# Attention softmax by single steps instead of doubles, with reciprocals ahead of older turns and x loads regrouped

## The chip, the cores and the metric

The kernel runs on one core of one Trainium2 chip. The metric is the device time of one execution in microseconds (us). The engines of the core run side by side, each through its own queue in order: TensorE (PE in the profile; its weight loads are PEld), VectorE (DVE), ScalarE (ACT), GpSimd (POOL) and SyncE (SP). SP computes nothing here; it issues most of the DMAs, POOL issues some. An instruction that waits holds up what is behind it on its own queue. PSUM is the memory into which TensorE writes[...]; SBUF is the memory that the others share.

## What is computed

Two layers on x, 4 images of 16 x 16 positions with 1024 channels, that is, 1024 tokens in 4 batches of 256. Everything is in float32. Layer 0 is a group norm, a convolution-like attention and a residual. Layer 1 is what the change is about, followed by a mixture of 8 experts:

```python
t = t + attn(ln(t), W_attn, b_attn, W_proj, b_proj)
...
qkv = einsum('btc,oc->bto', x, W_attn) + b_attn      # 16 heads of 64
att = einsum('bhqd,bhkd->bhqk', q, k) * (1.0 / sqrt(64))
att = where(causal, att, -1e29)
att = softmax(att, axis=-1)
y = einsum('bhqk,bhkd->bhqd', att, v)
y = einsum('btc,oc->bto', y, W_proj) + b_proj
```

## The kernel before

The stages follow each other: layer 0; layer norm and its turn (transposition of the rows); the products for v; then the stage of the change, attention with the q and k projections woven in; then the second layer norm, gating and lists; then the experts.

**The attention stage.** The 16 heads go as 8 pairs of heads. One pair in one batch is a *single step*: two heads, 256 queries, 256 keys. Two single steps are a *double*, and there are 16 doubles (`doubles`, lines 927 and 928): for the first six pairs a double is one pair in two batches, for the last two pairs it is both pairs in one batch. What happens to a double:

- `scores(d)` (line 817): TensorE writes q times k into one PSUM tile of four banks (line 824). VectorE adds the causal mask (838), takes two negated row maxima (843) and scales them (844). ScalarE takes eight exponentials into the SBUF tile s_q, with the row sums in total (848).
- `scored(d)` (858): VectorE takes the reciprocal of the sums (860), POOL multiplies s_q by it in eight pieces (863). SP then writes s_q to DRAM as one DMA of 768 KB (869) and reads it back by four DMAs of 192 KB (873) into s_rows, the quarters rearranged. The reads wait for the write.
- `turned(d)` (876): VectorE transposes s_rows in blocks of 32 x 32 into s_T (878).
- `values(d)` (884): TensorE multiplies v by s_T into the PSUM tile pa (891), VectorE adds the bias into y_T (900 or 909).

The tiles psc, s_q, s_rows and s_T have one buffer each, of the size of a double.

**The order.** The loop at line 940 is written out by hand (`manual_schedule`) and holds with step d work of three doubles: the turn of d - 2, the reciprocal, products and DMAs of d - 1, and the values of d - 2 and the scores of d. Each engine's order is the order of the text. Around these stand *units*: a unit is one of the seven products (in Strassen's way, on half-size blocks) of one pair's q and k projection, `project_qk` (779), four matmuls of 128 x 512 and an eviction on VectorE or ScalarE. A pair's product 4 is followed by the four sums of weights for the next pair, on VectorE (lines 160 to 163). `upto` (931) says how many units a step holds: 4, 3, 4, 3, 4, 4, 4, 4, 4, 3, 3, 5, 3 and 1 for steps 1 to 14. The units go through the PSUM tags mm and tr, two banks each; pa and the output projection use the same tags.

In each step the first two units come first, then the turn of d - 2, then the reciprocals and the DMAs of d - 1, then the other units, then values and scores. From step 14 on there are no units left and the output projection takes their place: `project_out(t, j)` (914), eight matmuls for 128 tokens and half of the columns, with `values_and_scores` called after its sixth. It adds its result to the tokens of x, which have been written to DRAM (x_rows) before and are loaded again in eight tiles of 512 KB by POOL's queue (968), two in step 14, two in step 15, four in step 16. Their SBUF space is that of the sums T and S of the projections, which must be done with. The weights of the output projection come in two halves, w_p0 in step 12 and w_p1 in step 14, on SP. Behind the loop (step 17 is the last) the gating stage begins; its first instructions on ScalarE and POOL wait until the last pa matmul is done, since they use that stage's space.

Of the kernel before, what the change touches and what calls it, by code (L numbers as in the profile page):

```python
# [32 lines left out]
F32 = mybir.dt.float32  # L33
# [6 lines left out]
P = 128  # L40
C = 1024
NC = C // P
# [3 lines left out]
NT = TOK // P  # L46
# [16 lines left out]
Q = 4  # L63
# [6 lines left out]
def kernel(  # L70
# [29 lines left out]
    def pool(stack, name, bufs=1, **kw):  # L100
        return stack.enter_context(tc.tile_pool(name=name, bufs=bufs, reuse_waits="tile", **kw))
# [545 lines left out]
    with ExitStack() as attention:  # L647
# [168 lines left out]

        def scores(d):

            psc = ps.tile([P, 4, HALF], F32, tag="sc", name=f"sc{d}", bufs=1)
            for k, (pair, b) in enumerate(doubles[d]):  # L820
                for qt in (1, 0):
                    for h in range(2):
                        part = slice(h * D, h * D + D)
                        nc.tensor.matmul(
                            psc[:, 2 * k + h, qt * P : qt * P + (qt + 1) * P],
                            qk[pair][part, 0, b * M + qt * P : b * M + (qt + 1) * P],
                            qk[pair][part, 1, b * M : b * M + (qt + 1) * P],
                            start=True,
                            stop=True,
                        )  # L830

            by_quarter = l1w.tile([P, Q, 12, 32], F32, tag="s_q", name=f"s_q{d}", bufs=1)

            def blocks(k, qt):
                return by_quarter[:, :, 3 * k + qt : 3 * k + 1 + 2 * qt, :].rearrange("p f b i -> p b f i")

            last = psc.rearrange("p k (t n) -> p k t n", t=2)[:, :, :, :P]
            nc.vector.tensor_add(last, last, mask.unsqueeze(1).unsqueeze(1).to_broadcast([P, 4, 2, P]))
            top = small.tile([P, 2, 4], F32, tag="top", name=f"top{d}")
            total = small.tile([P, 2, 4], F32, tag="total", name=f"total{d}")  # L840
            for qt in range(2):
                cols = slice(qt * P, qt * P + (qt + 1) * P)
                nc.vector.tensor_reduce(top[:, qt, :], psc[:, :, cols], AX.X, ALU.max, negate=True)
            nc.vector.tensor_scalar(top, top, 1.0 / D**0.5, None, ALU.mult)  # L844
            for k in range(4):
                for qt in range(2):
                    cols = slice(qt * P, qt * P + (qt + 1) * P)
                    nc.scalar.activation(  # L848
                        blocks(k, qt),
                        psc[:, k, cols].rearrange("p (b f i) -> p b f i", f=Q, i=32),  # L850
                        AF.Exp,
                        bias=top[:, qt, k : k + 1],
                        scale=1.0 / D**0.5,
                        accum_out=total[:, qt, k : k + 1],
                    )
            return blocks, total, by_quarter

        def scored(d, blocks, total, by_quarter):

            nc.vector.reciprocal(total, total)  # L860
            for k in range(4):
                for qt in range(2):
                    nc.gpsimd.tensor_mul(  # L863
                        blocks(k, qt),
                        blocks(k, qt),
                        total[:, qt, k : k + 1].unsqueeze(2).unsqueeze(3).to_broadcast([P, 1 + qt, Q, 32]),
                    )
            rows = turns.tile([P, Q, 12 * 32], F32, tag="rows", name=f"s_rows{d}")
            nc.sync.dma_start(rows.rearrange("q f r -> q (f r)"), by_quarter.rearrange("p f b i -> p (f b i)"))

            s_rows = l1w.tile([P, Q, 12 * 32], F32, tag="s_rows", name=f"s_rows{d}", bufs=1)
            for f in range(Q):
                nc.sync.dma_start(s_rows[ts(f, 32), :, :], rows[:, f, :].rearrange("(g j) r -> j g r", j=32))
            return s_rows

        def turned(d, s_rows):
            s_T = l1w.tile([P, 4, 3 * P], F32, tag="s_T", name=f"s_T{d}", bufs=1)
            nc.vector.transpose(  # L878
                s_T.rearrange("p k (b g j) -> p g (k b) j", b=3, g=Q),
                s_rows.rearrange("p g (b i) -> p g b i", i=32),  # L880
            )
            return s_T

        def values(d, s_T):

            pa = mm(f"pa{d}").rearrange("p (k n) -> p k n", k=2)
            for k, (pair, b) in enumerate(doubles[d]):
                g, off = pair // 2, (pair % 2) * P
                for kt in range(2):
                    for h in range(2):  # L890
                        nc.tensor.matmul(
                            pa[h * D : h * D + D, k, kt * P :],
                            v1[g][:, 2 * b + kt, off + h * D : off + (h + 1) * D],
                            s_T[:, 2 * k + h, 2 * kt * P : (kt + 2) * P],
                            start=(kt == 0),
                            stop=(kt == 1),
                        )
            (pair, b), (other, _) = doubles[d]
            if pair == other:
                nc.vector.tensor_scalar(  # L900
                    y_T[:, pair, b * M : (b + 2) * M],
                    pa.rearrange("p k n -> p (k n)"),
                    bv[:, pair : pair + 1],
                    None,
                    ALU.add,
                )
            else:
                for k, (pair, b) in enumerate(doubles[d]):
                    nc.vector.tensor_scalar(y_T[:, pair, ts(b, M)], pa[:, k, :], bv[:, pair : pair + 1], None, ALU.add)
# [17 lines left out]
        doubles = [((pair, b), (pair, b + 1)) for pair in range(pairs_in_turn) for b in (0, 2)]  # L927
        doubles += [((NPAIR - 2, b), (NPAIR - 1, b)) for b in range(B)]
        queue = [(pair, n) for pair in range(1, NPAIR - 2) for n in (1, 2, 6, 7, 4, 5, 3)]
        queue += [(pair, n) for some in ((1, 2, 6, 7, 4), (5, 3)) for pair in (NPAIR - 2, NPAIR - 1) for n in some]  # L930
        upto = (0, 4, 7, 11, 14, 18, 22, 26, 30, 34, 37, 40, 45, 48, 49)
        units = {d: queue[upto[d - 1] : upto[d]] for d in range(1, len(upto))}
        outs = {14: ((0, 0), (1, 0)), 15: ((2, 0), (0, 1)), 16: ((1, 1), (2, 1)), 17: ((3, 0),)}
        lag = 2
# [4 lines left out]
        with tc.manual_schedule():  # L939
            for d in range(len(doubles) + lag):  # L940
                if d % 4 == 0 and d < 12:
                    load_qk(d // 4 + 1)
                elif d == 12:
                    w_p.append(w_tile("w_p0", W_projT[:, :HALF]))

                def values_and_scores():
                    if d >= lag:
                        values(d - lag, turned_s.pop(d - lag))
                    if d < len(doubles):
                        made[d] = scores(d)  # L950

                ahead = units.get(d, ())
                for unit in ahead[:2]:
                    project_qk(*unit)
                if d >= lag:
                    turned_s[d - lag] = turned(d - lag, soft.pop(d - lag))
                if d - 1 in made:
                    soft[d - 1] = scored(d - 1, *made.pop(d - 1))
                for unit in ahead[2:]:
                    project_qk(*unit)  # L960
                if d == 14:
                    w_p.append(w_tile("w_p1", W_projT[:, HALF:]))
                    sums.close()
                    x_pool = pool(x_home, "xb", side="right")
                    xs = [x_pool.tile([P, C], F32, tag=f"x{t}", name=f"xb{t}") for t in range(NT)]
                    bp = pool(bp_home, "bp", side="right").tile([P, C], F32, tag="bp", name="bp")
                for t in {14: (0, 1), 15: (2, 3), 16: (4, 6, 5, 7)}.get(d, ()):
                    nc.gpsimd.dma_start(xs[t], x_rows[ts(t, P), :])
                if d == 15:
                    nc.gpsimd.dma_start(bp, b_proj.partition_broadcast(P))  # L970
                if d == 17:
                    for b, nt in tiles[NT - 2 :]:
                        nc.gpsimd.tensor_add(xs[2 * b + nt], xs[2 * b + nt], bp)
                if d in outs:
                    project_out(*outs[d][0], {NC - 3: values_and_scores}, True)
                    for out_of in outs[d][1:]:
                        project_out(*out_of, {}, True)
                else:
                    values_and_scores()
        share_banks("ps_rest", 3)  # L980
        bp_home.close()

# [738 lines left out]
```

## Time and profile before

| | us |
|---|---|
| median of 3 runs (lowest, highest) | 1237.92 (1236.72, 1238.04) |
| the profiled execution | 1239.31 |
| its span, first to last instruction | 1237.5 |
| attention loop, first scores to the end of the last values | 389.1 to 669.3 |
| VectorE busy in 389 to 671.2 | 152.8 of 282.2 |
| granted TensorE clock, mean of the span | 0.997 |

Mean durations in that stage: one 128 x 1536 transpose (878) 1775 ns; mask 1231 ns; the two maxima 691 and 1214 ns; one exponential 374 (128 x 128) or 484 ns (128 x 256), and 215 ns to read each sum; one eviction of 128 x 512 about 690 ns. From issue to landing, in the median, a write of s_q takes 3.3 us and a read of a quarter 3.8 us.

How to read the profile: an instruction's line is that of the kernel, and "x8" behind a row is how often it stands there. A float32 matmul leaves two records, so a unit is x8, values and scores x16. "[3.14 <-DMA s_rows<-s_rows]" means that the engine sat idle for 3.14 us before the instruction, and what ended that. A row of SPq or POOL with DMA_DIRECT2D is the issue of a DMA, not its transfer.

### The profile page before, as it was taken

The page shows a single profiled execution, that of the slowest core. Times are in us where ns is not written, and L with a number is a line of the kernel's source. Part 1 is how long each engine was busy: PE and PEld are TensorE (multiplying, and loading weights), DVE is VectorE, ACT ScalarE, POOL GpSimd, SP SyncE. Part 2 cuts the span into 40 slices and gives each one's busy share as a digit, 9 for nine tenths or more (in the row PEclk, how much of TensorE's full clock was granted, in tenths as well). Part 3 has the DMA queues.
Part 4 walks back from the last instruction along what each step waited for, and adds up shares of the span by engine and source line. Part 5 has one row for each costly group of instructions (what it writes and reads, how often), then busy time and mean ns, then how long its engine had stood idle before and what let it go on. Part 6 is the DMA issues. An engine that isn't in the chain of part 4 may idle for free.

```text
span 1237.5 us, 12955 instructions
## 1 busy us (share of the span) xinstructions
PE 1210.2 (98%) x4780; PEld 633.8 (51%) x4780; DVE 713.6 (58%) x1178; ACT 201.7 (16%) x502; POOL 404.5 (33%) x467
## 2 busy tenths in 40 slices
PE   9999999999999999999988999999999999999998
PEld 5445885778874445444443444444344434434443
DVE  5796636757323566566543567666656556565642
ACT  3310111120001222221210221101201111111110
POOL 0051341354000222133232016436442635364521
PEclk9999999999999999999999999999999999999999
DMA  9002014772210353535466755574855575556442
GB/s 348 24 1 77 10 50 141 242 249 69 68 53 15 103 170 102 171 102 168 126 191 179 250 175 186 153 222 89 239 144 158 111 229 162 142 147 183 100 83 54
DMA packets 82599, 169.75 MB, mean 137 GB/s; under 512 B 10688, under 2 KB 39376, under 8 KB 82528
## 3 DMA queue, kind: packets, MB, share of 16 engines
q1 hardware_dynamic: 62080, 108.48, 27.6%
q0 software_dynamic: 16144, 51.45, 17.3%
q10 hardware_dynamic: 4304, 8.91, 2.1%
q8 instruction: 40, 0.66, 0.2%
q14 instruction: 31, 0.25, 0.1%
HBM read 116.12 MB, written 48.50 MB: 133 GB/s over the span
## 4 chain that ended last, share of the span: by engine, by line
PE 81%; DMA 9%; DVE 3%; POOL 2%; issue 2%; SPq 2%; ACT 1%; DVEq 0%; POOLq 0%; ACTq 0%
PE p L1487 31%; PE pqk L665 13%; PE pv L665 7%; PE pq_pair L400 4%; PE left L1529 3%; PE pq L319 3%; PE pT L510 3%; DMA s_rows<-s_rows 3%; PE pk L431 2%; DMA ln_rows<-ln_rows 2%; PE pv L538 2%; DMA s_rows<-s_q 2%; POOL s_q L863 2%; PE rest L1543 2%; DMA quarters<-rows 2%
## 5 line engine op out<-in xcount | busy, mean ns | idle before, releaser
L1012 POOL DMA_INDIRECT w_e_xg<-rows,gather x146 | 155.5, 1065 | 50.9 <-issue 42.0
L1487 PE MATMUL p<-w_e,A 128*128 128x512 f32 x368 | 163.2, 593 | 1.3 <-DVE slot L1299 1.3
L863 POOL TENSOR_TENSOR s_q<-s_q,total 128x128 f32<-128x128 f32 (+1 forms) x128 | 63.6, 532 | 283.1 <-DVE total L860 283.1
L918 PE MATMUL po<-w_p,y_T 128*128 128x512 f32 x256 | 116.7, 606 | 0.0
L1035 POOL DMA_INDIRECT out_dram<-y,add x32 | 57.3, 1790 | 178.9 <-ACT y L1493 112.5
L1487 PEld LDWEIGHTS p<-w_e,A 128*128 128x128 f32 x368 | 69.6, 190 | 89.9 <-issue 89.0
L1487 PE MATMUL p<-T,S 128*128 128x512 f32 x256 | 112.7, 593 | 0.0
L1493 ACT ACTIVATE y<-y,slot 128x512 f32<-128x512 f32 x64 | 46.0, 721 | 331.1 <-DVE y L1501 152.7
L665 PE MATMUL pqk<-ln,w_qk 128*128 128x512 f32 x192 | 85.7, 595 | 0.0
L848 ACT ACTIVATE s_q<-sc,top 128x128 f32<-128x128 f32 (+1 forms) x128 | 51.8, 429 | 173.2 <-DVE top L844 101.4
L1487 PEld LDWEIGHTS p<-T,S 128*128 128x128 f32 x256 | 48.6, 190 | 60.8 <-issue 60.8
L918 PEld LDWEIGHTS po<-w_p,y_T 128*128 128x128 f32 x256 | 47.8, 193 | 54.5 <-issue 53.5
L187 DVE STREAM_TRANSPOSE A<-w_e_xg 128x1024 f32<-128x1024 f32 x32 | 39.6, 1238 | 48.6 <-DMA w_e_xg<-rows,gather 48.2
L665 PEld LDWEIGHTS pqk<-ln,w_qk 128*128 128x128 f32 x192 | 36.1, 190 | 43.7 <-issue 42.6
L665 PE MATMUL pqk<-T,S_qk 128*128 128x512 f32 x128 | 58.0, 595 | 0.0
L1487 PE MATMUL p<-T,A 128*128 128x512 f32 x128 | 57.5, 592 | 0.0
L1487 PE MATMUL p<-w_e,S 128*128 128x512 f32 x128 | 57.5, 592 | 0.0
L665 PE MATMUL pv<-w_v,ln 128*128 128x256 f32 x192 | 43.7, 380 | 2.1 <-ACT ln L223 1.1
L319 PE MATMUL pq<-w_q,xn 128*128 128x512 f32 x96 | 44.5, 600 | 0.3 <-ACT xn L299 0.3
L878 DVE STREAM_TRANSPOSE s_T<-s_rows 128x1536 f32<-128x1536 f32 x16 | 28.4, 1775 | 27.3 <-DMA s_rows<-s_rows 27.3
L1529 PE MATMUL left<-w_e,one 128*32 128x512 f32 x312 | 41.8, 593 | 0.0
L665 PEld LDWEIGHTS pv<-w_v,ln 128*128 128x128 f32 x192 | 36.2, 190 | 7.7 <-ACT ln L223 1.3
(329 smaller groups left out, 1823.5 us busy)
## 6 DMA issues: line engine op xcount, KB each, us to landing
w_e<-in_expert_w_dram SPq DMA_DIRECT2D x12, 2048.0 KB, 14.7
s_rows<-s_q SPq DMA_DIRECT2D x16, 768.0 KB, 3.3
s_rows<-s_rows SPq DMA_DIRECT2D x64, 192.0 KB, 3.8
w_qk<-in_W_attnT_dram SPq DMA_DIRECT2D x8, 1024.0 KB, 9.3
w_e<-in_expert_w_dram ACTq DMA_DIRECT2D x4, 2048.0 KB, 12.6
xn<-in_xT_dram SPq DMA_DIRECT2D x8, 512.0 KB, 7.2
w_q<-in_Wq_dram SPq DMA_DIRECT2D x16, 256.0 KB, 6.8
x_at<-in_x_dram POOLq DMA_DIRECT2D x8, 512.0 KB
```

The source lines that it names most:

```text
L187: nc.vector.transpose(row_T[:, :, :slots].rearrange("p c (g j) -> p g c j", j=32), row[:, : slots // 32, :].rearrange("p g (c i) -> p g c ...
L319: nc.tensor.matmul(pq, xn[:, c, ts(t, P)], w_q[kc][:, c, :], start=(c == 0), stop=(c == NC - 1))
L400: nc.tensor.matmul(bank, a[:, c, :], b[:, c, :], start=(c == 0), stop=(c == NC // 2 - 1))
L665: nc.tensor.matmul(bank, stationary(c), moving(c), start=(c == 0), stop=(c == NC // 2 - 1))
L848: nc.scalar.activation(blocks(k, qt), psc[:, k, cols].rearrange("p (b f i) -> p b f i", f=Q, i=32), AF.Exp, bias=top[:, qt, k : k + 1], sc ...
L863: nc.gpsimd.tensor_mul(blocks(k, qt), blocks(k, qt), total[:, qt, k : k + 1].unsqueeze(2).unsqueeze(3).to_broadcast([P, 1 + qt, Q, 32]),)
L918: nc.tensor.matmul(po, y_T[:, c, ts(t, P)], w_p[j][:, c, :], start=(c == 0), stop=(c == NC - 1))
L1012: nc.gpsimd.indirect_dma_start(out=row[:, g, :], out_offset=None, in_=table[: (TOK - P) * Q, :] if e in SHORT else table, in_offset=bass.I ...
L1035: nc.gpsimd.indirect_dma_start(out=out[: TOK - P, :] if e in SHORT else out, out_offset=bass.IndirectOffsetOnAxis(ap=add[:slots, e, k : k ...
L1487: nc.tensor.matmul(bank, a[:, c, :], b[:, c, :], start=(c == 0), stop=(c == NC // 2 - 1))
L1493: nc.scalar.mul(y[i][:, ts(j, HALF)], y[i][:, ts(j, HALF)], slot[:, e, 1, 2 * pair + i : 2 * pair + i + 1])
L1529: nc.tensor.matmul(bank[ts(i, 32), :], stationary, w[of][j][:, c, :], start=(c == 0), stop=(c == NC - 1))
```

## The change

- A double stays the unit of TensorE's products: the values, and the scores called for in one go. But the scores go into two PSUM tiles of two banks (tag sc, two buffers instead of one), and the softmax, the multiplication, the DMAs and the transposes go by single steps. s_q, s_rows and s_T have half the size and two buffers.
- A double thus has two writes of 384 KB and eight reads of 96 KB in place of one write and four reads, with the four reads of the first single step ahead of the write of the second on SP's queue. It has two reciprocals and two transposes, and VectorE's mask, maxima and scale twice at half the size.
- In steps 1 to 13 the turn of d - 2 comes after the first unit, not after the second.
- The last units are put in the order (6, 5), (7, 5), (6, 3), (7, 3); step 13 has two, step 14 two.
- In step 14 the reciprocals and DMAs of 13 come ahead of the turn of 12. The turn of 13 comes behind the first output projection of step 14, then the reciprocals of 14; the reciprocals of 15 come behind the second projection of step 15 and ahead of the turn of 14. In step 16 the values come with its second projection, not with its first.
- x is loaded as 0 and 1 in step 13, 2 and 3 in step 14, 4 and 6 in step 15, 5 and 7 in step 16.

The diff, cut to its core (`turned` and `values` follow the new names):

```diff
         def scores(d):
-            psc = ps.tile([P, 4, HALF], F32, tag="sc", name=f"sc{d}", bufs=1)
-            for k, (pair, b) in enumerate(doubles[d]):
+            banks = [ps.tile([P, 2, HALF], F32, tag="sc", name=f"sc{d}_{k}", bufs=2) for k in range(2)]
+            for psc, (pair, b) in zip(banks, doubles[d]):
...
+            return [softmax(f"{d}_{k}", psc) for k, psc in enumerate(banks)]
+
+        def softmax(name, psc):
+            by_quarter = l1w.tile([P, Q, 6, 32], F32, tag="s_q", name=f"s_q{name}")
...
+        def scored(name, blocks, total, by_quarter):
             nc.vector.reciprocal(total, total)
-            for k in range(4):
+            for h in range(2):
                 for qt in range(2):
                     nc.gpsimd.tensor_mul(
...
-            rows = turns.tile([P, Q, 12 * 32], F32, tag="rows", name=f"s_rows{d}")
+            rows = turns.tile([P, Q, 6 * 32], F32, tag="rows", name=f"s_rows{name}")
...
-        queue += [(pair, n) for some in ((1, 2, 6, 7, 4), (5, 3)) for pair in (NPAIR - 2, NPAIR - 1) for n in some]
-        upto = (0, 4, 7, 11, 14, 18, 22, 26, 30, 34, 37, 40, 45, 48, 49)
+        queue += [(pair, n) for some in ((1, 2, 6, 7, 4), (5,), (3,)) for pair in (NPAIR - 2, NPAIR - 1) for n in some]
+        upto = (0, 4, 7, 11, 14, 18, 22, 26, 30, 34, 37, 40, 45, 47, 49)
...
+                def go_on(at):
+                    if at - 1 in made:
+                        soft[at - 1] = [scored(*one) for one in made.pop(at - 1)]
+
+                def turn_back(at):
+                    if at >= lag:
+                        turned_s[at - lag] = [turned(*one) for one in soft.pop(at - lag)]
...
-                for unit in ahead[:2]:
-                    project_qk(*unit)
-                if d >= lag:
-                    turned_s[d - lag] = turned(d - lag, soft.pop(d - lag))
-                if d - 1 in made:
-                    soft[d - 1] = scored(d - 1, *made.pop(d - 1))
-                for unit in ahead[2:]:
-                    project_qk(*unit)
...
-                for t in {14: (0, 1), 15: (2, 3), 16: (4, 6, 5, 7)}.get(d, ()):
-                    nc.gpsimd.dma_start(xs[t], x_rows[ts(t, P), :])
...
+                if d < 14:
+                    for unit in ahead[:1]:
+                        project_qk(*unit)
+                    turn_back(d)
+                    go_on(d)
+                    for unit in ahead[1:]:
+                        project_qk(*unit)
+                    if d == 13:
...
+                        load_x(0, 1)
+                    values_and_scores(d)
+                elif d == 14:
+                    project_qk(*ahead[0])
+                    go_on(14)
+                    project_qk(*ahead[1])
+                    turn_back(14)
+                    w_p.append(w_tile("w_p1", W_projT[:, HALF:]))
+                    load_x(2)
+                    project_out(*outs[14][0], {NC - 3: lambda: values_and_scores(14)}, True)
+                    turn_back(15)
+                    project_out(*outs[14][1], {}, True)
+                    go_on(15)
+                    load_x(3)
+                elif d == 15:
+                    nc.gpsimd.dma_start(bp, b_proj.partition_broadcast(P))
+                    project_out(*outs[15][0], {NC - 3: lambda: values_and_scores(15)}, True)
+                    project_out(*outs[15][1], {}, True)
+                    go_on(16)
+                    load_x(4, 6)
+                    turn_back(16)
+                elif d == 16:
+                    project_out(*outs[16][0], {}, True)
+                    load_x(5, 7)
+                    project_out(*outs[16][1], {NC - 3: lambda: values_and_scores(16)}, True)
+                    turn_back(17)
```

## The prediction

> **What bounds the kernel now.** I read the page's engine line first, then TensorE's own waits, then the busy windows of the stretch in which those waits lie, then the timeline of that stretch.
>
> ```profile
> PE 1210.2 (98%) x4780; PEld 633.8 (51%) x4780; DVE 713.6 (58%) x1178; ACT 201.7 (16%) x502; POOL 404.5 (33%) x467
> PE pa L891 <- DVE s_T L878: 7.6, 3, 5.0
> PE pa L891 <- DVE total L860: 4.0, 2, 3.0
> ```
>
> TensorE is busy for all but 27.3 us of the 1237.5 us span, and the change adds and removes no matmul. So it can only pay in TensorE's idle time and in its clock. The two wait lines (total, times, longest) say where that is: 11.6 us, five times, in front of the attention values (pa, line 891). Both lines are one thing: the values wait for the turned probabilities s_T, and where the wait is put down to the reciprocal (line 860), it is only the instruction behind the transpose on VectorE.
>
> The windows hold steps 14, 15, 16 and 17 of the loop (columns: busy us of PE, PEld, DVE, ACT, POOL with instructions, granted clock, DMA share, GB/s):
>
> ```profile
> 591.48:608.70 17.22, 15.20 (x81) 7.94 (x81) 8.77 (x14) 3.33 (x16) 5.90 (x13) 1.00 0.32 92
> 608.70:626.40 17.70, 16.78 (x65) 8.25 (x64) 7.87 (x12) 3.33 (x16) 4.72 (x11) 1.00 0.90 262
> 626.40:646.00 19.60, 16.56 (x63) 7.93 (x59) 8.80 (x15) 4.81 (x18) 4.89 (x11) 0.99 0.61 166
> 646.00:671.20 25.20, 20.18 (x53) 9.28 (x54) 6.94 (x14) 1.33 (x2) 10.80 (x16) 0.87 0.53 146
> ```
>
> TensorE idles 2.0, 0.9, 3.0 and 5.0 us there; the fifth wait (0.6 us) is at 558.2, in step 11. The clock falls too. In stretches of 4 us it was 0.94 from 642, 0.63 from 646 and 0.57 from 666, after the two longest waits, and 1.00 elsewhere: 4 x (0.06 + 0.37 + 0.43) = 3.4 us. After the waits of 2.0 and 0.9 us it stayed at 1.00. At stake: 11.6 + 3.4 = **15.0 us**.
>
> Why the values wait shows in the last two steps:
>
> ```profile
> 642.39 1.78 DVE L878 STREAM_TRANSPOSE s_T<-s_rows 128x1536 f32<-128x1536 f32 x1 [3.14 <-DMA s_rows<-s_rows]
> 644.09 0.16 DVE L860 RECIPROCAL total<-total 128x8 f32<-128x8 f32 x1
> 644.32 1.68 PE L891 MATMUL pa<-s_T,v 128*64 128x256 f32 x16 [3.04 <-DVE total L860]
> 644.39 3.75 POOL L863 TENSOR_TENSOR s_q<-s_q,total 128x128 f32<-128x128 f32 x8 [14.71 <-DVE total L860]
> ...
> 648.09 2.16 POOL L968 DMA_DIRECT2D xb<-x_rows  x4
> 648.17 0.34 SPq L869 DMA_DIRECT2D s_rows<-s_q  x1
> ...
> 652.84 2.36 SPq L873 DMA_DIRECT2D s_rows<-s_rows  x4
> ...
> 664.60 1.78 DVE L878 STREAM_TRANSPOSE s_T<-s_rows 128x1536 f32<-128x1536 f32 x1 [7.61 <-DMA s_rows<-s_rows]
> ...
> 666.44 2.83 PE L891 MATMUL pa<-s_T,v 128*64 128x256 f32 x16 [5.02 <-DVE s_T L878]
> ```
>
> The reciprocal of double 15 stands on VectorE behind the transpose of double 14, which waits for its DMA. ScalarE had finished the exponentials of 15 at 636.2 (its last record of them), so double 15 lost 8 us by standing in that place. Then its DMAs ran into four x loads: write 4.67 us, reads 11.76 us until the transpose. A loop results: reciprocal, POOL products, write, four reads, transpose, next reciprocal. Its undisturbed length:
>
> ```profile
> 591.58 0.16 DVE L860 RECIPROCAL total<-total 128x8 f32<-128x8 f32 x1
> 591.82 3.75 POOL L863 TENSOR_TENSOR s_q<-s_q,total 128x128 f32<-128x128 f32 x8 [11.89 <-DVE total L860]
> 595.60 0.34 SPq L869 DMA_DIRECT2D s_rows<-s_q  x1
> 598.92 1.73 SPq L873 DMA_DIRECT2D s_rows<-s_rows  x4
> 604.61 1.78 DVE L878 STREAM_TRANSPOSE s_T<-s_rows 128x1536 f32<-128x1536 f32 x1 [4.61 <-DMA s_rows<-s_rows]
> 606.31 0.16 DVE L860 RECIPROCAL total<-total 128x8 f32<-128x8 f32 x1
> ```
>
> 4.02 to the write, 3.32 for it, 5.69 for the reads, 1.70 for the transpose: 14.73 us. A step of TensorE lasts 16.9 us with four projection products (13.93 + 1.45 values + 1.51 scores), 13.46 with three, 20.3 with five.
>
> **Part 1: single steps in the softmax and the turns.** Per double the same elements go through twice the instructions. VectorE: mask 1.23, two maxima 1.82, scale 0.17 become 2 x about (0.65 + 1.05 + 0.17), 0.5 us more; a second reciprocal, 0.16; two transposes of about 0.9 (a 128x1024 one took 1.25), nothing. VectorE idles 130 us of the 282 us of this stage, which hides it. POOL and ScalarE have the same pieces in halves.
>
> The DMAs are the price. SP issues write 0, four reads 0, write 1, four reads 1 in order, and the reads wait for their write, so write 1 stands behind it. A write of 384 KB isn't in the trace. Bounds: half of 3.32, or 3.32 unchanged. A write of 512 KB (rows<-row at 670.58) let its reads go after 3.15, so I take 3.0. [...] For the last read's landing after the four issues, 128 KB reads took 2.84 (675.46 to 678.30), the present 192 KB ones 3.96; I take 2.7 for 96 KB, with 3.96 above it[...].
>
> New loop: 0.24 + 1.88 (half the POOL work) + 0.04 = 2.16 to write 0; 3.0; issues 1.73 and 0.05; write 1 3.0; issues 1.73; landing 2.7; last transpose 0.9: **15.25 us**, 0.5 longer than now[...]. The second half of the values needs its half of s_T 0.7 us after the first, so TensorE tolerates that much more.
>
> Is it short enough? Step 2 (from 405.96) opens with product 4 and its 3.9 us of sums, so its reciprocals come at 416.1, as now. Adding 15.25 a step gives 431.4, 446.6, 461.9, 477.1, 492.4, 507.6 for steps 3 to 8, against values at 433.3, 446.8, 463.7, 480.6, 497.5, 514.4. Steps 9 and 10 are bound by their first product (523.5, 540.4), then 555.7 and 570.9 against 558.2 and 578.5. In step 13 (now two products, from 581.5) they come at 588.3 for values at 588.5. Steps 4 and 13 are tight: I charge 0.5 us there; the 0.6 us wait of step 11 goes. While a transpose waits, the evictions of products 2 to 4 stand behind it on VectorE. Four banks turn over, each reused four products later (13.7 us), so TensorE does not follow. At one product earlier in the order (part 2) the transposes are also off the 9.5 us floor of now (reciprocal 591.58, step from 582.1); the new floor is about 6.2.
>
> **Part 2: the order of the last steps.** In step 14 the reciprocals of 13 stand in front of the transposes of 12, later ones behind a projection but never behind their predecessor's late DMA. Step 14 starts at 591.5. Reciprocals of 12 came at 588.3; their last transpose would be done at 603.5, for values at 603.7. x loads 0 and 1, issued behind POOL's products at 592.3, lie in between. Now, such a pair made the write 4.76 instead of 3.32 and the reads 7.30 instead of 5.69, 3.1 us in all; here only part of the DMAs meets it: 0 to 3.1, I take a wait of **1.0**. Double 13: its writes queue on SP behind 12's last reads (601), turned by about 616, values at 622. Double 14: reciprocals 617, turned by 634 with w_p1 in flight, values at 645. Double 15: reciprocals 634 (now 644), write 0 636, reads 639, write 1 641, with the x loads 645, reads until 650 (alone) to 656 (delayed as now); values at 653.5, half of them 0.7 later. Wait 0 to 2.5; I take **0.7**.
>
> **Part 3: x in smaller portions.** Loads 4, 6 and 5, 7 are two groups in the text, but nothing on POOL waits between them, so they go back to back as now. Only their place changes: 638 instead of 648, behind the products of 15. Issues cost POOL 0.55 each with nobody behind. Units (6, 5) and (7, 5) move ahead of both (3), which frees T for x 0 and 1 in step 13. No cost on TensorE.
>
> **Sum.** 15.0 - 0.5 - 1.0 - 0.7 = **12.8 us**. Short waits cost no clock by the rows above. The profiled execution took 1239.31 (span 1237.5 and 1.8 around it); it would take 1226.5. It lies 1.4 above the median of the runs, 1237.92, which gives **1225.1**.
>
> **Rivals.**
> - *The last turn still meets the x loads* (chance 0.15). If the reads of double 15 again need 11.8 us from about 646, s_T is there at 659 and TensorE waits 4.5 us and loses 1.7 in clock: 1225.1 + 5.5 = about 1230.6. For: the load order is unchanged in effect. Against: the first half's DMAs are ahead of the loads.
> - *The loop over SP becomes the bound* (0.12; slower). Steps 2 to 12 average 15.95 us. A loop of L us costs 11 x (L - 15.95). The 12.8 us are gone at L = 17.1, which is 1.9 above my sum. Two turns of now took 16.5 and 17.2 us (from 526.85 and 558.70), when POOL needed 5.5 instead of 3.75 beside VectorE's sums of weights. At L = 17.7 it costs 19: about 1244. Against: the reciprocals now come before those sums in steps 7 and 9.
> - *The change doesn't remove the waits, merely moves them* (0.05): double 13's DMAs behind 12's on SP push 14 and 15 back until all four waits return: about 1238. Against: 5 to 10 us of margin for 13 and 14.
>
> **The numbers.** The forecast's own case has 0.68 and reaches from 1222.5 (all 15.0 us and noise) to 1228. The range goes to 1233, to hold the first rival and loops a little too long. By over 0.2% (2.5 us, about what a measurement of this kernel can tell from no change): faster 0.84 (0.68 + 0.15 and a hundredth of the loop), within 0.05, slower 0.11 (the rest of the loop).
>
> **What would show it.** Right: TensorE's waits at pa under 3 us; clock 1.00 through the stage; scores and values of step 13 ending near 591; last values near 654 instead of 666; second transposes about 5 us behind first ones; reciprocal to reciprocal at 15 to 15.5 us in steps 3 to 8. Wrong: equal waits of one to two us in every step of three products (the loop), write 1 over 4 us undisturbed, or one long wait in front of the last values.

## The result and the profile after

| | before | after |
|---|---|---|
| median of 4 runs each, side by side (us) | 1237.98 | 1224.81 |
| lowest, highest | 1236.72, 1240.94 | 1222.15, 1227.45 |
| ratio, 95% interval | | 0.989 (0.986 to 0.992) |
| profiled execution, its span | 1239.31, 1237.5 | 1227.45, 1225.6 |
| first scores to the first POOL instruction behind the last values | 389.01 to 669.34 = 280.3 | 389.32 to 655.90 = 266.6 |

The changed kernel is 13.2 us faster. In a second comparison, with five rounds, the ratio was 0.9875 (0.9853 to 0.9898). The last row of the table is the length of the attention stage in the profile; it is free of what other stages do, and I use it below to tell kernels apart. It fell by 13.7 us.

The engine line of the page after, and the two rows of its DMA issues that belong to the change (size of each, median us from issue to landing):

```profile
PE 1208.7 (99%) x4780; PEld 632.8 (52%) x4780; DVE 721.4 (59%) x1274; ACT 203.8 (17%) x502; POOL 401.5 (33%) x467
...
s_rows<-s_q SPq DMA_DIRECT2D x32, 384.0 KB, 2.3
s_rows<-s_rows SPq DMA_DIRECT2D x128, 96.0 KB, 2.3
```

TensorE's idle time is 16.9 us instead of 27.3. VectorE has 7.8 us more work, 0.49 per double, and it hid it all. A write of half the size lands in 2.3 us, where the whole one took 3.3.

TensorE's waits after: the row that heads the list now, which lies behind the stage, and the only one at pa:

```profile
PE lists L1287 <- POOL entry L1276: 2.8, 3, 1.9
...
PE pa L893 <- DVE s_T L880: 0.9, 2, 0.6
```

Of the 11.6 us in front of pa, 0.9 are left, both in step 14 (0.30 and 0.56 us, one for each half). The windows of steps 14 to 17, cut at the same instructions as before (columns as before; the clock is the number ahead of the DMA share):

```profile
591.78:608.11 16.33, 15.47 (x63) 7.59 (x61) 7.93 (x17) 3.44 (x16) 6.03 (x13) 1.00 0.68 218
608.11:625.00 16.89, 16.89 (x67) 8.28 (x65) 8.42 (x18) 3.44 (x16) 4.81 (x10) 1.00 0.76 249
625.00:645.79 20.79, 20.79 (x50) 9.03 (x48) 10.33 (x24) 4.93 (x18) 8.78 (x14) 1.00 0.59 183
645.79:657.60 11.81, 11.81 (x54) 5.83 (x54) 5.13 (x10) 1.33 (x2) 3.46 (x4) 1.00 0.40 123
```

Span and busy time of PE agree from 608.11 on, and the clock is 1.00 in all four. The last values start at 654.31 instead of 666.44.

SP's own rows of double 15, the last one. They show what is left of the trouble with the x loads:

```profile
636.66 0.34 SPq L871 DMA_DIRECT2D s_rows<-s_q  x1
639.05 1.73 SPq L875 DMA_DIRECT2D s_rows<-s_rows  x4
640.88 0.85 SPq L871 DMA_DIRECT2D s_rows<-s_q  x1
649.84 1.73 SPq L875 DMA_DIRECT2D s_rows<-s_rows  x4
```

The reads wait for their write, so the distance between a write's row and the next row is that write's time. Write 0 took 2.39 us. POOL began to issue the four x loads at 638.46; write 1, from 640.88, took 8.96 us. In steps 1 to 12 write 1 took 2.57 to 3.09 us, 2.65 in the median. The second half of s_T was ready at 654.54, half a microsecond before its matmuls were due.

### The profile page after: what moved, and what is told of

Its sections match the earlier page's. It is cut to its first block, busy times and chain, and to the rows that moved or that the text cites. A ratio compares the mean times of both kernels' runs of the same rounds, so it can differ in the third digit from the quotient of the medians.

```text
span 1225.6 us, 13283 instructions
## 1 busy us (share of the span) xinstructions
PE 1208.7 (99%) x4780; PEld 632.8 (52%) x4780; DVE 721.4 (59%) x1274; ACT 203.8 (17%) x502; POOL 401.5 (33%) x467
## 4 chain that ended last, share of the span: by engine, by line
PE 87%; DMA 7%; DVE 3%; SPq 2%; issue 1%; ACT 1%; POOL 0%; DVEq 0%; POOLq 0%; ACTq 0%
PE p L1516 31%; PE pqk L665 15%; PE pv L665 7%; PE po L920 5%; PE pq_pair L400 4%; PE left L1558 3%; PE pq L319 3%; PE pT L510 3%; DMA ln_rows<-ln_rows 2%; PE pk L431 2%; PE sc L824 2%; PE pa L893 2%; PE rest L1572 2%; PE pv L538 2%; DMA quarters<-rows 1%; DMA s<-two_T 1%
## 5 line engine op out<-in xcount | busy, mean ns | idle before, releaser
L865 POOL TENSOR_TENSOR s_q<-s_q,total 128x128 f32<-128x128 f32 (+1 forms) x128 | 60.2, 506 | 276.5 <-DVE total L862 276.5
L1516 PEld LDWEIGHTS p<-w_e,S 128*128 128x128 f32 x128 | 24.3, 190 | 30.6 <-issue 30.1
L1516 PEld LDWEIGHTS p<-T,A 128*128 128x128 f32 x128 | 24.3, 190 | 30.6 <-issue 30.1
```

What stands on the lines that cost most here:

```text
L865: nc.gpsimd.tensor_mul(blocks(h, qt), blocks(h, qt), total[:, qt, h : h + 1].unsqueeze(2).unsqueeze(3).to_broadcast([P, 1 + qt, Q, 32]),)
L1516: nc.tensor.matmul(bank, a[:, c, :], b[:, c, :], start=(c == 0), stop=(c == NC // 2 - 1))
```

## The experiments

Ratios are to the kernel before on the same chip in the same comparison, with the 95% interval. "Stage" is the length defined above: 280.3 us before, 266.6 after.

**1. The order alone, whole doubles.** Functions of the kernel before, loop of the changed kernel:

```diff
-soft[at - 1] = [scored(*one) for one in made.pop(at - 1)]
+soft[at - 1] = scored(at - 1, *made.pop(at - 1))
-turned_s[at - lag] = [turned(*one) for one in soft.pop(at - lag)]
+turned_s[at - lag] = turned(at - lag, soft.pop(at - lag))
```

> The whole doubles of the kernel before, with one buffer each, in the order of the changed kernel (units, reciprocals ahead of older turns, places of the x loads). Theory A, the order of the last steps gives the gain: most of it stays. Two of TensorE's waits at pa should come back in part, because a whole double meets the x loads with all of its DMAs: in step 14, 0.5 to 2.4 us; in front of the last values, 2 to 3 us (reciprocals 634.5, write at 638.3 with the x loads beside it, 4.7 for the write and 11.8 to the transpose as in the kernel before, turned at 656.4 for values planned at 654.3), with up to 1 us of clock. 1224.8 + 3.5 = about 1228 us, from 1225 to 1231. Theory B, the cutting into single steps gives it: the waits at pa return to about 10 us or more, 1235 us or above.

Measured: 1231.41 us, ratio 0.994 (0.9924 to 0.9957), stage 273.2. TensorE's waits at pa:

```profile
PE pa L891 <- DVE s_T L878: 5.2, 2, 3.0
```

The two waits are where they were expected, 2.96 us in step 14 and 2.28 in front of the last values. The clock fell behind both, by 3.4 us in 4 us windows together (0.69 and 0.88 in 604 to 612, 0.57 in 660 to 664), more than I had allowed. A wait of 0.8 us for ScalarE in step 6 is new. The time lies just above the range that I had given. So most of what theory A said holds, but the order alone is worth 7.2 us of the 13.7, and the cutting is worth something too.

**2. The single steps alone, old order.** Functions of the changed kernel, `queue`, `upto` and loop of the kernel before.

> The single steps of the changed kernel, with two buffers each, in the order of the kernel before (two units ahead of the turns, turns of d-2 ahead of the reciprocals of d-1 everywhere, x loads in steps 14 to 16). Theory A, the order gives the gain: the reciprocals of 15 stand behind both transposes of 14 again, the second of which comes 4.5 us behind the first, so the reciprocals come at 644 or later, the writes meet four x loads, and the last values wait 5 us or more, with clock lost behind it: 1236 to 1242 us, as before or slower. Theory B, the single steps give it: waits at pa under 3 us, 1228 us or less.

Measured: 1232.83 us, ratio 0.9948 (0.993 to 0.9966), stage 274.4. This lies between my two theories, and A's number was wrong: single steps help in the old order too, by 5.9 us. Waits at pa are 5.5 us in all (the longest 3.51, the last half of the last values), and a new one of 1.78 us stands in front of an output projection, for w_p1: SP issued that load at 619.32, behind more DMAs. The reciprocals of 15 did come late, at 641.8, and write 0 started at 644.0, before the x loads of 645.8, but its reads already met them. Only 0.9 us separated the first half of the last values from its plan; the second half was the late one.

**3. One pair of the order undone.** In step 15:

```diff
-                    go_on(16)
-                    load_x(4, 6)
-                    turn_back(16)
+                    turn_back(16)
+                    go_on(16)
+                    load_x(4, 6)
```

> The changed kernel with one pair swapped: in step 15 the reciprocals, products and DMAs of double 15 stand behind the transposes of 14 again, and so do the x loads 4, 6, 5, 7. Theory A, the reciprocal's place is what removed the longest wait: reciprocals at 639.1 instead of 634.5, write 0 at 641.2, write 1 at 645.4 beside the x loads (8.9 us as in the changed kernel), reads, landing and transpose until 658.4; the last values, planned at 654.3 and by halves 0.7 later, wait 3 to 3.7 us, and 0 to 2 us of clock go with it: about 1229 us, from 1227 to 1231. Theory C, the place does not matter as long as the DMAs are cut: no wait, 1225 us.

Measured: 1228.87 us, ratio 0.992 (0.9902 to 0.9937), stage 270.1, 3.5 longer than after. TensorE's rows at the end of the stage:

```profile
653.17 0.87 PE L893 MATMUL pa<-s_T,v 128*64 128x256 f32 x8
657.60 0.87 PE L893 MATMUL pa<-s_T,v 128*64 128x256 f32 x8 [3.56 <-DVE s_T L880]
```

The first half is in time, the second waits 3.56 us, as theory A worked out. The reciprocals stood at 637.4 here, write 1 took 9.0 us once more. Where the reciprocal of 15 stands is worth 3.5 us by itself.

**4. Both writes ahead of all reads.** In the changed kernel, `scored` ends behind its write, and the reads follow for both single steps:

```diff
-soft[at - 1] = [scored(*one) for one in made.pop(at - 1)]
+written = [scored(*one) for one in made.pop(at - 1)]
+soft[at - 1] = [read_back(*one) for one in written]
```

> The changed kernel with both writes of a double issued ahead of its eight reads on SP, instead of write, reads, write, reads. My step on the price: write 1 stands behind the four reads of single step 0, so this order shortens the loop by about 1.8 us (write 1 issued at 4.0 us behind the reciprocal, when the POOL products are done, landing at about 7; reads 1 done issuing at 9.0, landed at 11.7, turned at 12.6 instead of 14.4). VectorE's waits for s_rows in steps 3, 5 and 11 (now 4.6, 4.9 and 0.5 us for both transposes) fall by 1.5 to 2 us each, the last transpose of a double comes 2 to 3 us behind the first instead of 4.2 to 4.5. On TensorE only the 0.9 us of waits in step 14 can go: 1224 us, from 1223 to 1225.5, not to be told from the changed kernel. Rival: two writes in flight share the DMA engines, write 0 lands about 1 us later, and the loop keeps its length; the time is the same, 1224.8.

Measured: 1223.51 us, ratio 0.9878 (0.9861 to 0.9894), stage 265.7, no wait at pa. SP's rows of one loop:

```profile
415.60 2.20 SPq L871 DMA_DIRECT2D s_rows<-s_q  x2
418.00 5.09 SPq L878 DMA_DIRECT2D s_rows<-s_rows  x8
```

The reads may go 2.40 us after the first write (2.46 in the changed kernel). But SP issued the second write only at 417.46, when POOL's products for it were done, so the two were in flight together for 0.54 us; what two writes cost each other over their whole length, no run here shows. This loop had its reciprocals at 413.46 and 425.87, 12.4 us apart (14.45 in the changed kernel for the same pair of doubles), and the second transpose came 2.2 us behind the first. In step 5, the other loop in which VectorE waited for both transposes, it was 13.1 against 14.7. The price of SP's order is thus real, 1.6 to 2.0 us a loop, and almost nothing waits for it: the time is that of the changed kernel.

**5 and 6. A longer loop.** The reads issued twice, for both single steps of a double (5, shown here) or for the first alone (6, where the doubling has the condition `name.endswith("_0")`); same data, same place:

```diff
-            for f in range(Q):
+            for f in 2 * tuple(range(Q)):
```

> The changed kernel with the four reads of every single step issued twice (the same data into the same place), to lengthen the loop over SP by what eight more issues take, 2 x 1.73 = 3.5 us. The rival of my prediction that is slower says: in the changed kernel the loop is 14.4 us from reciprocal to reciprocal where nothing disturbs it, TensorE's steps 2 to 12 average 15.95, so a loop of 17.9 us costs 11 x (17.9 - 15.95) = 21 us: about 1246 us, from 1238 to 1256, with waits at pa in nearly every step from 3 to 13, of 1 to 5 us, and more clock lost. If TensorE is not near this bound (theory D: the loop is hidden by the two buffers), the time stays under 1230 us.

> The changed kernel with the reads issued twice for the first single step of each double alone: four more issues, 1.73 us, and a loop of about 16.2 us. By the same sum 11 x (16.2 - 15.95) = 3 us: 1227.5 us, from 1225 to 1231, with waits at pa where two shorter steps follow each other (from step 9 on). Above 1238 us would mean that the break-even lies lower than the 17.1 us of my prediction.

Measured: with all reads doubled 1284.32 us, ratio 1.0371 (1.0351 to 1.0392), and with the first single step's alone 1247.0, ratio 1.0074 (1.0051 to 1.0096). The direction is the rival's, the size is far more. Part of it is the loop: the extra issues took longer than 1.73 us (eight reads in a row took 4.06 us to issue at 452.11 in 6 and 5.41 at 497.45 in 5, where twice 1.73 makes 3.46), and on average from reciprocal to reciprocal it was 19.3 us (416.27 to 590.25, nine times) and 17.1 (411.64 to 582.68, ten times), against my 17.9 and 16.2. The rest shows in the second kernel's waits:

```profile
PE pa L893 <- DVE total L862: 7.1, 3, 3.6
PE pa L893 <- DVE s_T L880: 6.7, 3, 3.4
PE pa L893 <- DVE qk L802: 3.7, 1, 3.7
```

With one of 0.8 that makes 18.3 us. By step: 8.7 up to step 11, where my formula gives 11 x (17.1 - 15.95) = 12.7; 9.6 in steps 13, 14 and 17, which the formula leaves out (2.89, 3.33 and 3.38); and the clock lost 8.5 us behind them, in five falls of 1.7 us each by 4 us windows. With all reads doubled, TensorE waited 44 us at pa and the mean clock fell from 0.997 to 0.979.

**7 and 8. The x loads behind the reads.** Loads 0, 1, 4, 6, 5, 7 go to SP's queue in the same places of the text, so behind the reads of doubles 12 and 15; once in the changed kernel, once in the kernel of experiment 1, with whole doubles:

```diff
-                        nc.gpsimd.dma_start(xs[t], x_rows[ts(t, P), :])
+                        (nc.gpsimd if t in (2, 3) else nc.sync).dma_start(xs[t], x_rows[ts(t, P), :])
```

> The changed kernel with x loads 0, 1 and 4, 6, 5, 7 issued by SP, behind the reads of doubles 12 and 15, instead of by POOL between the two writes. Theory E, the loads held up the second write: write 1 of double 15 then lands 2.7 us behind its issue instead of 9.0, and its transpose ends at about 649.5 instead of 654.5; write 1 of double 12 takes 2.7 instead of 5.75, and the two waits of step 14 (0.9 us together) go. No wait at pa is left: 1224 us, ratio 0.988 to the kernel before. Rival: the delay was another's (the writes themselves, or the weights w_p1), and the second write is as late as before.

> The whole doubles of the kernel before with one buffer each, in the changed order (as in the experiment with the order alone, which gave 0.994 of the kernel before), and x loads 0, 1 and 4, 6, 5, 7 issued by SP behind the reads. Theory E, what the single steps were worth is only that fewer DMAs meet the x loads: then double 12 is turned at 602.7 for values planned at 603.1, double 15 at about 647.5 for values at 652, and both waits (3.0 and 2.3 us) and the clock behind them (3.4) go: ratio about 0.988, like the changed kernel, without a single step in it. Theory F, the cutting itself or the second buffers are worth the difference: the ratio stays at 0.993 to 0.995, with 4 us or more of waits at pa.

Measured: with single steps 1225.23 us, ratio 0.9896 (0.9881 to 0.9911), stage 265.4, no wait at pa. Write 1 of 15 took 2.70 us instead of 8.96 (issued at 639.79, reads at 642.49), write 1 of 12 took 2.86 instead of 5.75. With whole doubles 1224.57 us, ratio 0.9885 (0.987 to 0.99), stage 266.5. The waits of the whole doubles, and SP's rows of double 15:

```profile
PE pa L891 <- ACT qk L800: 0.8, 1, 0.8
...
PE pa L891 <- DVE s_T L878: 0.2, 1, 0.2
```

```profile
636.16 0.34 SPq L869 DMA_DIRECT2D s_rows<-s_q  x1
639.48 1.73 SPq L873 DMA_DIRECT2D s_rows<-s_rows  x4
641.25 2.33 SPq L962 DMA_DIRECT2D xb<-x_rows  x4
```

The write takes 3.32 us again, the transpose comes at 647.48, and the last values, at 651.92, wait for nothing. In experiment 1 the same double, beside the same loads, had its transpose at 657.08. So a kernel without a single step in it is as fast as the changed one: theory E. Between experiments 7 and 8 the stage differs by 1.1 us, 0.8 of it the wait for ScalarE in step 6. One rival is left. On SP's queue the loads also start later: 5.1 us behind the write of double 15 here, where in experiment 1 POOL started them with it (640.72, the write at 640.80). Whether POOL's queue would do as well with loads as late, no run here shows.

**9 and 10. What was given back behind the stage.** In the first profile after, the list matmuls waited 1.85 us at 702.1, and the clock was 0.62 from 704 to 708. One entry of the order of the later stage, moved ahead, puts tile 2's entries ahead of a transpose that waits for its DMA, in the changed kernel (9) and in that of experiment 4 (10); the changed kernel ran beside them once more:

```diff
-            47: ((1, 4),),
-            48: ((7, 0), (6, 2)),
+            47: ((6, 2), (1, 4)),
+            48: ((7, 0),),
```

> The changed kernel once more, as the measure for the other three: 0.989 of the kernel before, about 1225 us, waits at pa of about 0.9 us in step 14.

> The changed kernel with one edit behind the attention stage: the entries of tile 2 of the lists (VectorE's two comparisons, POOL's two products) stand ahead of the transpose of tile 4's rows on VectorE, which waits for its DMA. Theory G, part of the gain was given back there: in the changed kernel that transpose waited 4.9 us, the entries stood behind it, the list matmuls waited 1.85 us for them, and in its profiled execution the clock fell to 0.62 for 4 us behind that wait. Then the wait of 1.85 us goes and the clock stays at 1.00: 1.9 to 3.6 us less than the changed kernel, about 1222.5, from 1221 to 1224. Rival: the wait only moves to the matmuls of tile 4's rows a little later, and the time stays at 1225.

> Both edits together: both writes of a double ahead of its reads (which left no wait at pa) and the entries of tile 2 ahead of the transpose that waits for its DMA. By theory G and the sum of the two: 0.9 us for the waits of step 14 and 1.9 to 3.6 for the lists, so 1221.5 us, from 1220 to 1223.5, the fastest of all, ratio to the kernel before 0.986 to 0.987.

Measured: 1223.09, 1223.15 and 1223.78 us; ratios 0.9875 (0.9853 to 0.9898), 0.9864 (0.9845 to 0.9883) and 0.9876 (0.9855 to 0.9897). Theory G falls, and kernel 10 was not the fastest: no kernel tried is faster than the changed one by more than these intervals tell. In kernel 9 the lists' waits were 0.9 us (2.8 and 2.4 in the two profiles of the changed kernel), but the matmuls of tile 4's rows now waited 1.0 us. In the second profile of the changed kernel the wait of 1.85 us was one of 1.51 and the clock stayed at 1.00 there, so the dip does not come in every execution; behind the same wait, it came in experiments 7 (1.81 us; 0.98 and 0.59 from 696 to 704) and 8 (1.95 us; 0.60 and 0.97 from 700 to 708) and not in 4 (1.94 us; 1.00). Kernel 10 had a wait of 1.36 us at pa in step 14 where experiment 4, with the same loop, had none in its list of waits. In both, double 12 meets x loads 0 and 1; why it was later in kernel 10 is open.

**11. The kernel before, with four loads moved.** Only loads 4, 6, 5, 7 go to SP, behind the reads of double 15:

```diff
-                    nc.gpsimd.dma_start(xs[t], x_rows[ts(t, P), :])
+                    (nc.gpsimd if t < 4 else nc.sync).dma_start(xs[t], x_rows[ts(t, P), :])
```

> The kernel before, untouched but for x loads 4, 6, 5, 7, which SP issues behind the four reads of double 15 instead of POOL behind its products. Theory E, the loads held the last turn up: reciprocals at 644.1 as before, write at 648.2 lands in 3.3, reads issued at 651.5, turned at 658.9 for values that could start at 661.4; the wait of 5.0 us goes, and the 1.7 us of clock behind it. The other four waits stay (6.6 us, 3.0 the longest). 1238 - 6.7 = 1231.3 us, from 1230 to 1233, ratio 0.9946: half of the gain of the whole change by one queue. Rival, the late reciprocal alone made the wait: 3 us or more of it stay, 1235 us or above.

Measured: 1233.28 us, ratio 0.9942 (0.9925 to 0.9958), stage 274.4. What is left of the waits:

```profile
PE pa L891 <- DVE s_T L878: 2.8, 2, 2.1
PE pa L891 <- DVE total L860: 2.6, 1, 2.6
```

The wait of 5.0 us is gone though the reciprocal is as late as ever (645.23): its write took 3.32 us, the transpose came at 658.30 instead of 664.60, and the values at 662.48 did not wait. Four loads moved to another queue are worth 6.0 us of the stage. The clock lost 3.4 us as before: a dip behind the wait of 2.1 us in step 14 (0.57 in 608 to 612), which had cost no clock in the kernel before, took the place of the one behind the last values, and the wait of 0.9 us in step 15 went with it, since TensorE, slowed by the dip, came to it later. So the 1.7 us of clock that I had counted on did not come in this execution.

## Why the prediction was right, point by point

- **What is at stake** (15.0 us: waits at pa and clock). Right. 10.7 of the 11.6 us of waits went, and all 3.4 of clock. In the stage 13.7 us arrived.
- **The loop over SP** (15.25 us). Too long by 0.5 to 0.8. VectorE waited for both transposes in two loops, and these took 14.45 us (415.02 to 429.47) and 14.72 (445.36 to 460.08). The first of them:

```profile
415.02 0.20 DVE L862 RECIPROCAL total<-total 128x4 f32<-128x4 f32 x2
417.16 0.34 SPq L871 DMA_DIRECT2D s_rows<-s_q  x1
419.62 2.69 SPq L875 DMA_DIRECT2D s_rows<-s_rows  x4
422.41 0.38 SPq L871 DMA_DIRECT2D s_rows<-s_q  x1
424.99 1.73 SPq L875 DMA_DIRECT2D s_rows<-s_rows  x4
428.57 0.98 DVE L880 STREAM_TRANSPOSE s_T<-s_rows 128x768 f32<-128x768 f32 x1 [3.23 <-DMA s_rows<-s_rows]
```

Three terms were mis-sized, and in part they cancel. The writes took 2.46 and 2.58 us, not 3.0 each. The last read landed 1.85 us after the four issues, not 2.7. The issues of the first four reads took 2.8 us until the second write could go, not 1.78; in undisturbed steps they took 1.8, and what held them up here is open. Cutting cost less than my rows had it: two halves take 2.4 + 2.7 - 3.3 = 1.8 us more than a whole, where 2 x 3.0 - 3.3 makes 2.7. Of a write's time, 2 x 2.4 - 3.3 = 1.5 us did not shrink with its size, an estimate from the 3.3 us for a whole and 2.4 for a half.
- **Steps 4 and 13** (0.5 us). Nothing waited. In step 4 the reciprocals came 1.2 us earlier than forecast, since the loop is shorter. In step 13 they came as forecast (588.45), 0.37 us ahead of the values: that held, but only just.
- **VectorE** (0.5 us per double, hidden). Right: 0.49, hidden.
- **Step 14** (1.0 us). 0.86, from where it was put: write 1 of 12 took 5.75 us beside x loads 0 and 1.
- **Step 17** (0.7 us). No wait. The collision was there as described (write 1 at 641, reads until past 650), but the second transpose was done at 654.54, half a microsecond in time. That it cost nothing is luck within the range that I had given (0 to 2.5 us). The first rival was that close; the order of one pair, undone in experiment 3, brings it about.
- **What does it.** Here the prediction was only half right. It put down the gain to the order and charged the single steps as a price. The order alone gave 7.2 us of stage, the single steps alone 5.9, both 13.7. The single steps' share is what my remark against the first rival says, that the first half's DMAs are ahead of the loads, and I left it out of the sum as a gain. Experiments 7 and 8 show that this is nearly their whole share: with the x loads on POOL, single steps make the stage 6.6 us shorter (experiment 1 against the changed kernel), with the loads behind the reads 1.1 us. Nor is the late reciprocal the one cause of the longest wait, as the reading of the last two steps suggests: experiment 11 leaves it late and loses the wait.
- **The slower rival** (break-even at L = 17.1). Its mechanism is shown, its price was too low. At 17.1 us, in experiment 6, the kernel is not level with the one before but 8.9 us slower. The step that failed is "11 x (L - 15.95)": it counts steps 2 to 12 alone, and the short steps 13 to 17 and the clock took twice as much as those steps (9.6 + 8.5 against 8.7 us). A straight line between the changed kernel (14.45, 13.2 us faster) and experiment 6 (17.1, 8.9 slower) puts the break-even near 16; if a loop costs nothing up to the mean step of 15.95, it lies near 16.6. Both are estimates, and rough, since 14.45 is one loop and 17.1 the mean of ten. So with the loop of 15.25 us that the prediction reckoned with, the margin was 0.8 to 1.4 us and not 1.9. The real loop was shorter, and that made up for it by luck.
- **"Short waits cost no clock by the rows above."** This held in the changed kernel's stage, where no wait was longer than 0.56 us. But the length of a wait alone did not decide it: a wait of 2.0 us cost nothing before, one of 1.85 us behind the stage cost 1.7 us after. The last section has more such pairs.

Without the two charges that did not come due (0.5 and 0.7 us) the sum would have been 14.0 us. The interval of the ratio, 0.986 to 0.992, is a gain of 10 to 17 us at 1238 us, so it does not tell 12.8 from 14.0; the stage's 13.7 lies nearer to the latter. That the forecast of 1225.1 us lies only 0.3 from the median of 1224.81 is therefore in part luck: the gain in the stage was 0.9 us larger than the sum.

## What to carry to other kernels

When a chain of dependent DMAs feeds the engine that bounds the kernel, look first at what another queue starts beside it. Here a bulk load that nobody waited for tripled a write's time (2.7 to 9.0 us), and issuing four such loads behind the chain's reads on the same queue did nearly half of what the whole change did (6.0 of 13.7 us). Price a longer loop at the shortest steps that it meets, not at the mean step, and add the clock that waits cost, here 1.7 us for most dips.

## What was not expected of the hardware

- Four loads of 512 KB on POOL's queue stretched a write of 384 KB on SP's queue from 2.7 us to 9.0, in three kernels alike (the changed one, experiments 2 and 3). The same loads on SP's queue, behind the reads, left it at 2.70 (experiment 7).
- TensorE's granted clock fell behind some waits and not behind others of much the same length. Three waits of the values in step 14 or 16 and four of the lists, with the clock in 4 us windows:

| | wait (us), and where it ended | clock behind it |
|---|---|---|
| before | 2.02, 606.44 | 1.00 (604 to 612) |
| experiment 11 | 2.10, 607.39 | 0.57 (608 to 612) |
| before | 3.04, 644.32 | 0.69, 0.88 (644 to 652) |
| after | 1.85, 702.10 | 0.96, 0.62 (700 to 708) |
| experiment 4 | 1.94, 699.79 | 1.00 (696 to 708) |
| experiment 7 | 1.81, 699.36 | 0.98, 0.59 (696 to 704) |
| experiment 8 | 1.95, 699.81 | 0.60, 0.97 (700 to 708) |

What decides between the two, no run here shows. What a fall costs is alike: by such windows 1.7 us each time in the kernel before (twice), in the first profile after, and in experiments 1 (twice), 3, 7, 8 and 11 (twice); 3.4 us in experiment 2, and up to 5.1 in experiment 5, where waits follow each other. Cut into slices of 0.1 us, the clock in the kernel before was 0.50 from 645.6 to 648.9 and from 666.1 to 669.4, and 1.00 on either side.
